# Two graph layers on one core: layer 1 of 20 row blocks moves beside the last product, its late rows listed on the chip

## The chip, the core and the metric

The kernel runs on one core of a Trainium2 chip. A core has five engines that run side by side, each through its own list of instructions in order: TensorE (PE, with its weight loads shown as PEld), VectorE (DVE), ScalarE (ACT), GpSimd (POOL) and SyncE (SP), which here only issues transfers. An engine waits for another through semaphores. 16 DMA engines move data between device memory and the on-chip memory (SBUF); results of TensorE land in PSUM. The metric is the time of one launch on the device, in microseconds (us).

## The reference, cut to what matters

```
x   : 2708 x 512, adj : 2708 x 2708 (about 0.3% of the entries, and the diagonal, are not zero; values 0.05 to 1)

# layer 0
d   = rowsum(adj) ** -0.5
out = relu( (d[:,None] * adj * d[None,:]) @ x @ W + b )
h   = layernorm(x + out)

# layer 1 (4 heads, then their mean)
xn     = h @ W_node + b_node
feats  = einsum('nd,hdf->hnf', xn, K)
logits = s[:, :, None] + (-1e10) * (1 - adj)        # s is one number for each head and row
attn   = softmax(logits, over the columns)
out    = mean over heads of (attn @ feats)
y      = layernorm(h + relu(out))
```

In layer 1 the term with -1e10 decides the softmax: where the largest entry of a row of adj stands clear of the next, the weight of its column is 1 and all others are 0, for every head. Row i of attn @ feats is then feats[j], where j is the column of the largest entry of row i. With M = W_node times the mean of K over the heads, row i of layer 1 is u[j] with u = h @ M + c, so the layer is a gather of rows of u.

## The kernel before, in words

The 2708 rows are split into two halves of 1354, and each half into 10 blocks of 128 rows and one of 74. Block `ib` is part `ib // 2` of half `ib % 2`, so there are 22 blocks; blocks 20 and 21 have 74 rows. "Late" rows below are those of blocks 20 and 21: positions 1280 to 1353 of each half.

**Setup** (up to about 120 us): all of adj and x is loaded, x @ W is formed block by block (`v`), row sums are taken, and M (`m_sb`) and c (`c_bc`) are built from W_node, K and b_node.

**Main loop.** The product adj @ v is made two row blocks at a time. `m` (0 to 10) counts the pairs, `k` (0 to 10) the pairs of column blocks, and one step (m, k) does, in the order in which it is written out by hand (`manual_schedule`; nothing is reordered):
- `ahead(i + 2)`: four transposes of adj blocks for the step after the next (line 289), a copy out of PSUM on ACT (L291), four sums on DVE (L296 to L299). So the sums of a step are needed two steps later.
- `products(i)`: seven products of 128x256 (L318), instead of eight, into four PSUM banks.
- on DVE one piece of `todo`: the layer norm of the pair before (`rows_1`, `rows_2`, `rows_3`), or `scan`, which finds the largest entries of half a row block and their positions (L379, L380).
- at k = 7 and 8 the finished rows h of the pair before are transposed (`turn`), and after the last k `combine` puts the seven products together and `store_u` multiplies h of the pair before by M (L162, 16 matmul records a block pair) and stores u to device memory (`u_d`).

`rows_2` sends the variance to POOL, which adds epsilon and raises to -0.5 (L366, L367), and `rows_3` waits for it.

**After the loop** the last pair (blocks 20 and 21) goes through `rows_1` to `rows_3`, `turn` and `store_u`. A small matmul sums the flags of rows whose maximum does not stand clear (L491); if there were any, a dense version of layer 1 would run at the end. Then layer 1 proper runs for all 22 blocks: POOL issues one indirect transfer for each block, which fetches the rows u[j] (`fetch_row`, L508); DVE applies relu and adds h (L518), takes the statistics (L520, L521); POOL raises four columns at a time to -0.5 (`spread`, L526); ACT normalizes (L536) and SP stores the block to the output. The h of blocks 0 to 9 is read back from device memory (`reload_h`) at the second step of the last pair, that of blocks 10 to 19 after the loop. The column numbers j (`indices`) are computed on DVE at k = 8 of the last pair.

Of the kernel before, what the change touches and what calls it, by code (L numbers as in the profile page):

```python
# [44 lines left out]
GAP = -200.0  # L46


@with_exitstack
def tile_two_graph_layers(  # L50
# [26 lines left out]
    SHORT = rows(NB - 1)  # L77

# [27 lines left out]

    nc.sync.dma_start(out=w_sb, in_=W.rearrange("(c p) o -> p c o", p=P))
# [3 lines left out]
    half_neg = const.tile([P, 4], F32, name="half_neg")  # L111
# [10 lines left out]
    idx = const.tile([P, NB], U32, name="idx")  # L122
    bad_i = const.tile([1, 1], I32, name="bad_i")
    nc.vector.memset(sums, 1.0)
    nc.vector.memset(top, 0.0)
    nc.vector.memset(at, 0)

# [145 lines left out]

    mix = ctx.enter_context(tc.tile_pool(name="mix", bufs=1, side="right"))
# [107 lines left out]
    def store_u(ib):  # L382
        pr = rows(ib)
        po = times(hTs.pop(ib), pr, m_sb)
        ut = mix.tile([P, D], F32, name="ut", bufs=2)
        nc.vector.tensor_add(ut[:pr], po[:pr], c_bc[:pr])  # L386
        store(u_d, ut, ib)

    def indices():


        def col():
            return small.tile([P, NB], F32, name="col", bufs=8)

        v0, v1 = top[:, :, 0, 0], top[:, :, 1, 0]
        best, nxt, tmp = col(), col(), col()
        nc.vector.tensor_tensor(best, v0, v1, op=ALU.max)
        nc.vector.tensor_tensor(nxt, v0, v1, op=ALU.min)
        nc.vector.tensor_tensor(tmp, top[:, :, 0, 1], top[:, :, 1, 1], op=ALU.max)
# [4 lines left out]
        bad = col()  # L404
        nc.vector.memset(bad, 0.0)
        nc.vector.tensor_scalar(bad[:, : NB - 2], nxt[:, : NB - 2], GAP, None, op0=ALU.is_ge)
        nc.vector.tensor_scalar(bad[:SHORT, NB - 2 :], nxt[:SHORT, NB - 2 :], GAP, None, op0=ALU.is_ge)
        bad1 = small.tile([P, 1], F32, name="bad1")
        nc.vector.tensor_reduce(bad1, bad, axis=AX.X, op=ALU.max)
        sel, fa, fb = col(), col(), col()  # L410
        nc.vector.tensor_tensor(sel, v1, v0, op=ALU.is_gt)
        nc.vector.tensor_copy(fa, at[:, :, 0, 0])
        nc.vector.tensor_copy(fb, at[:, :, 1, 0])
        nc.vector.tensor_sub(fb, fb, fa)
        nc.vector.scalar_tensor_tensor(fb, fb, float(HALF), sel, op0=ALU.add, op1=ALU.mult)
        nc.vector.tensor_add(fa, fa, fb)
        nc.vector.tensor_copy(idx, fa)
        return bad1
# [3 lines left out]
    hres = {}  # L422

    def reload_h(lo, hi):
        for ib in range(lo, hi):
            if (ib - lo) % PER == 0:
                hold = apool.tile([P, N], F32, name="a")
            n = (ib - lo) % PER
            hres[ib] = hold[:, n * D : (n + 1) * D]
            load(hres[ib], h_d, ib)  # L430
# [4 lines left out]
    bad1 = None  # L435
    for i, (m, k) in enumerate(steps):
        at_k = i % NM
        if at_k == 0:
            banks = [p_p.tile([P, 2, FH], F32, name=f"bank{n}") for n in range(4)]
            todo = []  # L440
            if done is not None:
                for q in range(2):
                    todo.append([lambda ib=2 * (m - 1) + q, t=done[q]: rows_1(ib, t)])
                    todo.append([lambda ib=2 * (m - 1) + q, t=done[q]: rows_2(ib, t)])
                todo[3].append(lambda ib=2 * (m - 1), t=done[0]: rows_3(ib, t))
                todo.append([lambda ib=2 * (m - 1) + 1, t=done[1]: rows_3(ib, t)])
            look = [(2 * m + 2 + q, hf, 1, q) for q in range(2) for hf in range(2)] if m + 1 < NM else []
# [5 lines left out]
            if m == NM - 1:  # L453
                todo.append([lambda: None])
# [9 lines left out]
        if done is not None and at_k in (7, 8):  # L464
            q = at_k - 7
            hTs[2 * (m - 1) + q] = turn(done[q], rows(2 * m - 2), nc.scalar.copy)
        if m == NM - 1 and at_k == 1:
            reload_h(0, 2 * PER)
        if m == NM - 1 and at_k == 8:
            bad1 = indices()  # L470
# [17 lines left out]
    for q in range(2):  # L488
        store_u(2 * last + q)
# [155 lines left out]
```

## Time and profile before

| | |
|---|---|
| time, median of 3 runs | 696.97 us (695.75 to 698.27) |
| time of the profiled execution | 699.27 us |
| its span, first to last instruction | 697.4 us |
| TensorE busy | 616.2 us, 88% of the span |
| VectorE busy | 462.0 us |
| ScalarE busy | 157.0 us |
| GpSimd busy | 71.6 us |
| last product of the main loop ends | about 613 us |
| first gather is issued | 643.15 us |
| last output store is issued | 692.6 us |

Busy time of an engine is the time in which the profile shows an instruction running on it. An average over the span hides the stages: up to 120 us the transfers are the limit, from there to about 620 us TensorE runs without a gap, and after that it has little to do. The clock that was granted to TensorE is shown as a share of full speed; it is 1 in the main loop and 0.5 in parts of the end.

### The profile page before, as it was taken

How to read it: one execution, taken by the hardware profiler on the slowest of the kernel's cores; microseconds unless marked ns; L12 is line 12 of the kernel's file. 1: busy time of each engine (PE TensorE's matmuls, PEld its weight loads, DVE VectorE, ACT ScalarE, POOL GpSimd, SP SyncE). 2: the span in 40 equal slices, each digit the busy share in tenths (PEclk: the TensorE clock that was granted, in tenths of full speed). 3: DMA queues.
4: the chain of work that ended last, by engine and by line, in shares of the span. 5: the costliest groups of instructions: out<-in, count | busy, mean ns of one | idle time of the engine just before them, and what ended most of it. 6: DMA issues, size and time to landing. Idle time of an engine off the chain costs nothing.

```text
span 697.4 us, 7653 instructions
## 1 busy us (share of the span) xinstructions
PE 616.2 (88%) x2768; PEld 456.6 (65%) x2768; DVE 462.0 (66%) x1116; ACT 157.0 (23%) x221; POOL 71.6 (10%) x102
## 2 busy tenths in 40 slices
PE   5999979999999999999999999999999999965000
PEld 3545434887878878878788788787887876731000
DVE  1356886998776856858659578586595775350693
ACT  2544455211111211211111112111121111100054
POOL 0011321000001001000010000000100001010771
PEclk9999999999999999999999999999999999986555
DMA  8999799013050230400513204014041105013785
GB/s 350 412 391 404 299 360 338 1 63 128 30 205 30 108 128 31 189 32 32 204 46 141 80 31 190 31 68 182 31 101 53 62 15 188 28 39 101 250 285 182
DMA packets 29892, 101.79 MB, mean 146 GB/s; under 512 B 3904, under 2 KB 3904, under 8 KB 24688
## 3 DMA queue, kind: packets, MB, share of 16 engines
q1 hardware_dynamic: 27608, 95.69, 37.2%
q0 software_dynamic: 2240, 5.55, 2.6%
q8 instruction: 23, 0.38, 0.2%
q14 instruction: 21, 0.17, 0.1%
HBM read 84.59 MB, written 16.64 MB: 145 GB/s over the span
## 4 chain that ended last, share of the span: by engine, by line
PE 78%; DVE 12%; DMA 4%; POOL 3%; issue 1%; ACT 1%; SPq 0%
PE bank L318 48%; PE po L162 21%; PE tp L289 6%; PE tp L154 3%; DMA gt<-u_d,idx 2%; DVE at L380 2%; POOL gt L508 2%; DVE top L379 2%; DVE km L241 1%; DMA v<-in_x_dram 1%; PE po L265 1%; DVE v L181 1%; DVE aT L299 1%; ACT gt L536 1%; DVE st L520 1%
## 5 line engine op out<-in xcount | busy, mean ns | idle before, releaser
L318 PE MATMUL bank<-v,aT 128*128 128x256 f32 (+3 forms) x968 | 268.5, 380 | 0.3 <-DVE t L340 0.3
L318 PE MATMUL bank<-t,aT 128*128 128x256 f32 (+3 forms) x726 | 196.5, 379 | 1.2 <-DVE u L345 0.8
L318 PEld LDWEIGHTS bank<-v,aT 128*128 128x128 f32 (+3 forms) x968 | 170.6, 186 | 22.4 <-DVE t L340 0.6
L318 PEld LDWEIGHTS bank<-t,aT 128*128 128x128 f32 (+3 forms) x726 | 134.8, 186 | 23.7 <-DVE u L345 1.2
L291 ACT COPY aT<-tp 128x512 f32<-128x512 f32 (+3 forms) x121 | 68.9, 570 | 347.9 <-PE tp L289 334.4
L296 DVE TENSOR_TENSOR aT<-aT 128x128 f32<-128x128 f32 (+3 forms) x121 | 33.8, 279 | 88.1 <-ACT aT L291 88.1
L162 PE MATMUL po<-w_sb,sT 128*128 128x512 f32 (+1 forms) x176 | 80.9, 604 | 3.3 <-DVE sT L156 3.3
L162 PE MATMUL po<-m_sb,sT 128*128 128x512 f32 (+1 forms) x176 | 80.2, 610 | 0.0
L289 PE MATMUL tp<-ident,a 128*128 128x128 f32 (+3 forms) x484 | 70.5, 269 | 0.3 <-ACT aT L291 0.3
L379 DVE MAX8 top<-a 128x8 f32<-128x1354 f32 (+1 forms) x44 | 68.8, 1563 | 0.0
L380 DVE FIND_INDEX8 at<-top,a 128x8 uint32<-128x1354 f32 (+1 forms) x44 | 68.7, 1562 | 0.0
L289 PEld LDWEIGHTS tp<-ident,a 128*128 128x128 f32 (+3 forms) x484 | 58.6, 139 | 15.2 <-issue 5.3
L235 ACT ACTIVATE junk<-a 128x2708 bf16<-128x2708 f32 (+1 forms) x22 | 54.1, 2461 | 48.5 <-DMA a<-in_adj_dram 48.5
L162 PEld LDWEIGHTS po<-m_sb,sT 128*128 128x128 f32 (+1 forms) x176 | 33.4, 190 | 40.2 <-issue 39.6
L366 POOL TENSOR_SCALAR rs<-mv 128x1 f32<-128x1 f32 (+1 forms) x22 | 7.5, 342 | 481.0 <-DVE mv L364 481.0
L162 PEld LDWEIGHTS po<-w_sb,sT 128*128 128x128 f32 (+1 forms) x176 | 31.7, 190 | 37.5 <-issue 33.5
L386 DVE TENSOR_TENSOR ut<-po,c_bc 128x512 f32<-128x512 f32 (+1 forms) x22 | 15.2, 691 | 50.8 <-PE po L162 50.8
L233 DVE COPY v<-po 128x512 f32<-128x512 f32 (+1 forms) x22 | 15.2, 690 | 35.3 <-PE po L162 35.3
L299 DVE TENSOR_TENSOR aT<-aT 128x128 f32<-128x128 f32 (+3 forms) x121 | 34.6, 286 | 4.2
L297 DVE TENSOR_TENSOR aT<-aT 128x128 f32<-128x128 f32 (+3 forms) x121 | 33.7, 278 | 0.0
L298 DVE TENSOR_TENSOR aT<-aT 128x128 f32<-128x128 f32 (+3 forms) x121 | 33.7, 278 | 0.0
L175 POOL TENSOR_TENSOR dinv<-dinv,half_neg 128x1 f32<-128x1 f32 x22 | 19.0, 863 | 102.7 <-DVE dinv L174 102.7
(90 smaller groups left out, 372.4 us busy)
## 6 DMA issues: line engine op xcount, KB each, us to landing
a<-in_adj_dram SPq DMA_DIRECT2D x38, 1354.0 KB, 6.1
v<-in_x_dram SPq DMA_DIRECT2D x20, 256.0 KB, 10.5
xr<-in_x_dram SPq DMA_DIRECT2D x20, 256.0 KB, 8.9
h_d<-t SPq DMA_DIRECT2D x20, 256.0 KB, 2.1
u_d<-ut SPq DMA_DIRECT2D x20, 256.0 KB
a<-h_d SPq DMA_DIRECT2D x20, 256.0 KB, 4.5
out_dram<-gt SPq DMA_DIRECT2D x20, 256.0 KB, 3.7
kh<-in_L_gnn_K_dram SPq DMA_DIRECT2D x3, 1024.0 KB
```

The costliest lines, as they stand in the source:

```text
L154: nc.tensor.transpose(ps[:, f, :pr], src[:pr, f * P : (f + 1) * P], ident[:pr, :pr])
L162: nc.tensor.matmul(po[:pr], sT[:, f, :pr], wt[:, f, :], start=(f == 0), stop=(f == ND - 1))
L235: nc.scalar.activation(junk[:pr], a[:pr], AF.Copy, accum_out=sums[:pr, ib : ib + 1])
L289: nc.tensor.transpose(ps[:kr, q, :pr], raw[m][q // 2][:pr, lo : lo + kr], ident[:pr, :pr])
L291: nc.scalar.copy(aT[:kr, :4, :pr], ps[:kr, :, :pr])
L296: nc.vector.tensor_add(s(S1), s(L21), s(L22))
L297: nc.vector.tensor_sub(s(S3), s(L11), s(L21))
L298: nc.vector.tensor_sub(s(S2), s(S1), s(L11))
L299: nc.vector.tensor_sub(s(S4), s(L12), s(S2))
L318: nc.tensor.matmul(banks[bank][:pr, side, :], aT[:kr, left, :pr], right, start=first and side == 0, stop=last, skip_group_check=True,)
L379: nc.vector.max(out=top[:pr, ib, hf, :], in_=part)
L380: nc.vector.max_index(out=at[:pr, ib, hf, :], in_max=top[:pr, ib, hf, :], in_values=part)
```

## The change

Layer 1 of blocks 0 to 19 is done while the last pair (m = 10) is still being multiplied, except for the rows that need a row u[j] of blocks 20 or 21.

- `u` is stored with relu applied (one more ACT instruction a block), and the gather adds to h in place: h of a block is loaded into its place (`home`), and the indirect transfer has `compute_op=add`. The DVE pass L518 is gone. The device tensors `u_d` and `out` are each seen as two views, early and late, which are not ordered against each other.
- At m = 9, `marks` (k = 1) computes the column numbers of blocks 0 to 19, sets the number of a row that needs a late row to 0, and flags it. Two small matmuls count the flags; `ranks` (k = 2) turns the counts into a running number for each flagged row; `enlist` (k = 3 to 7, four blocks a step) makes on POOL a 128x256 matrix with a one at the row's number (`hot`, two buffers) and on TensorE two matmuls of it with a table `about` of each row's coordinates, so that up to 256 rows are listed in PSUM; `listed` (k = 9) turns the list into three columns of addresses: which row of h, which row of u, which row of the output.
- At m = 10 the layer norm of blocks 18 and 19 is drawn together into the first two steps, `turn` comes at k = 2 and `store_u` of 18 and 19 at k = 3. POOL then fetches blocks 0 to 4 at k = 4, 5 to 9 at k = 5, 10 to 14 at k = 7 and reads h of the listed rows at k = 8; DVE takes the statistics of blocks 0 to 4 at k = 7 and of 5 to 9 at k = 9; the first five blocks are normalized and stored at k = 8.
- After the loop come the last pair's layer norm and `store_u`, blocks 15 to 19, then the gathers of blocks 20 and 21 and a second gather for the 256 listed places, whose normalized rows are scattered over the rows that were stored before. Places that stand for no row carry an address past the end and are dropped.
- Before the loop, blocks 20 and 21 of `h_d` and `u_d` are filled with `b_bc`, so that every row can be read.

```diff
+    NE = NB - 2
+    LATE = (NM - 1) * P
+    NL = CAP // P                      # CAP = 256
+    u_early, u_late = dram_disjoint_views(u_d[:, :], 2)
+    out_early, out_late = dram_disjoint_views(out, 2)
...
+    for ib in (NE, NE + 1):
+        for t in (h_d, u_d):
+            store(t, b_bc, ib)
...
         nc.vector.tensor_add(ut[:pr], po[:pr], c_bc[:pr])
-        store(u_d, ut, ib)
+        nc.scalar.activation(ut[:pr], ut[:pr], AF.Relu)
+        store(u_late if ib >= NE else u_early, ut, ib)
...
+    def marks():
+        sel, pos_in, full = indices(0, NE, P)          # 15 DVE operations on 20 columns
+        flag = small.tile([P, NE], F32, name="flag", bufs=1)
+        nc.vector.tensor_scalar(flag, pos_in, float(LATE), None, op0=ALU.is_ge)
+        nc.vector.scalar_tensor_tensor(full, pos_in, float(LATE), full, op0=ALU.is_lt, op1=ALU.mult)
+        nc.vector.tensor_copy(idx[:, :NE], full)
+        nc.vector.tensor_scalar(about[:, :, 3], pos_in, float(LATE), None, op0=ALU.subtract)
+        nc.vector.tensor_copy(about[:, :, 4], sel)
+        flag_b = small.tile([P, NE], BF16, name="flag_b", bufs=1)
+        nc.vector.tensor_copy(flag_b, flag)
+        ps = p_o.tile([P, D], F32, name="po")
+        nc.tensor.matmul(ps[:, :NE], before, flag_b, start=True, stop=True)
+        nc.tensor.matmul(ps[:, NB : NB + NE], every, flag_b, start=True, stop=True)
+        return flag, ps
+    def ranks(flag, ps):
...
+        while shift < NE:                              # 5 rounds
+            a, t = runs[n], runs[1 - n]
+            nc.vector.tensor_add(t[:, PAD:], a[:, PAD:], a[:, PAD - shift : PAD - shift + NE])
...
+    def enlist(rank, ls, bl):
+        for ib in bl:
+            hot = mix.tile([P, CAP], BF16, name="hot", bufs=2)
+            nc.gpsimd.tensor_scalar(hot, place, rank[:, ib : ib + 1], None, op0=ALU.is_equal)
+            for n in range(NL):
+                nc.tensor.matmul(ls[:, n * 6 : n * 6 + 6], hot[:, n * P : (n + 1) * P], about[:, ib, :],
+                    start=(ib == 0 and n == 0), stop=(ib == NE - 1), skip_group_check=True)
...
+    def home(c):                                       # h of five blocks into one buffer
+        t = mix.tile([P, N], F32, name="home") if c == 2 else apool.tile([P, N], F32, name="a")
+        for n, ib in enumerate(range(c * PER, (c + 1) * PER)):
+            gt[ib] = t[:, n * D : (n + 1) * D]
+            load(gt[ib], h_d, ib)
+    def fetch_row(ib):
+        pr = rows(ib)
+        fetch(gt[ib], pr, idx[:pr, ib : ib + 1], u_d if ib >= NE else u_early, compute_op=ALU.add)
+    def chunk_stats(c):                                # DVE: statistics of 5 blocks; POOL: power of 5 columns
+        for ib in range(*chunk(c)):
+            stats(ib, P)
+        spread(*chunk(c))
+    def chunk_out(c):                                  # DVE: shift (waits for POOL); ACT: normalize; SP: store
+        shift_of(*chunk(c))
+        for ib in range(*chunk(c)):
+            normalize(ib, P)
+            store(out_early, gt[ib], ib)
...
+        if m == NM - 2:                                # m = 9, after products() and the todo piece
+            if at_k == 1:
+                flag, ps = marks()
+            elif at_k == 2:
+                rank = ranks(flag, ps)
+                ls = p_o.tile([P, D], F32, name="po")
+            elif 3 <= at_k < 8:
+                per = NE // 5
+                enlist(rank, ls, range((at_k - 3) * per, (at_k - 2) * per))
+            elif at_k == 9:
+                to_read, to_get, to_put = listed(ls)
+        if final:                                      # m = 10
+            if at_k == 0:
+                home(0)
+                home(1)
+            elif at_k == 1:
+                home(2)
+            elif at_k == 2:
+                for q in range(2):
+                    hTs[2 * (m - 1) + q] = turn(done[q], P, nc.scalar.copy)
+            elif at_k == 3:
+                store_u(NE - 2)
+                store_u(NE - 1)
+            elif at_k == 4:
+                sel, pos_in, full = indices(NE, NB, SHORT)
...
+                for ib in range(*chunk(0)):
+                    fetch_row(ib)
+            elif at_k == 5:
...
+                for ib in range(*chunk(1)):
+                    fetch_row(ib)
+            elif at_k == 7:
+                chunk_stats(0)
+                for ib in range(*chunk(2)):
+                    fetch_row(ib)
+            elif at_k == 8:
+                chunk_out(0)
+                for n in range(NL):
+                    gt[NB + n] = mix.tile([P, D], F32, name=f"again{n}")
+                    fetch(gt[NB + n], P, to_read[:, n : n + 1], h_d)
+            elif at_k == 9:
+                chunk_stats(1)
+            elif at_k == 10:
+                home(3)
         if at_k == NM - 1:
-            if done is not None:
-                new = combine(m, banks)
+            new = combine(m, banks)
+            if done is not None and not final:
                 store_u(2 * m - 2)
                 store_u(2 * m - 1)
...
+    chunk_out(1)
+    for q in range(2):
+        rows_1(NE + q, done[q])
+        rows_2(NE + q, done[q])
+    for ib in range(*chunk(3)):
+        fetch_row(ib)
+    for q in range(2):
+        rows_3(NE + q, done[q])
+        hTs[NE + q] = turn(done[q], SHORT, nc.scalar.copy)
+    chunk_stats(2)
+    store_u(NE)
+    first, after = chunk(3)
+    for ib in (first, first + 1):
+        stats(ib, P)
+    store_u(NE + 1)
+    for ib in range(first + 2, after):
+        stats(ib, P)
+    spread(first, after)
+    for q in range(2):
+        gt[NE + q] = done[q]
+        fetch_row(NE + q)
+    for n in range(NL):
+        fetch(gt[NB + n], P, to_get[:, n : n + 1], u_late, compute_op=ALU.add)
+    chunk_out(2)
+    chunk_out(3)
+    for ib in (NE, NE + 1):
+        stats(ib, SHORT)
+    spread(NE, NB)
+    for n in range(NL):
+        stats(NB + n, P)
+    spread(NB, NB + NL)
...
+    for n in range(NL):
+        normalize(NB + n, P)
+        nc.gpsimd.indirect_dma_start(out=out_early[:, :],
+            out_offset=bass.IndirectOffsetOnAxis(ap=to_put[:, n : n + 1], axis=0),
+            in_=gt[NB + n], in_offset=None, bounds_check=N - 1, oob_is_err=False)
```

## The prediction

> **What bounds the kernel now.** I read the stages first (busy time by window: PE, PEld, DVE, ACT, POOL, then TensorE clock, DMA share, GB/s).
>
> ```profile
> 500.00:550.00 50.00, 50.00 (x245) 41.17 (x244) 34.17 (x83) 8.49 (x16) 1.78 (x4) 1.00 0.31 78
> 620.00:640.00 20.00, 11.24 (x26) 4.08 (x26) 7.46 (x15) 0.81 (x2) 2.60 (x4) 0.74 0.17 43
> 640.00:660.00 20.00, 0.00 (x0) 0.00 (x0) 9.33 (x20) 0.00 (x0) 13.19 (x13) 0.50 0.80 265
> 660.00:680.00 20.00, 0.00 (x0) 0.00 (x0) 18.79 (x44) 8.78 (x12) 16.03 (x14) 0.50 0.85 269
> 680.00:698.00 18.00, 0.00 (x0) 0.00 (x0) 5.96 (x16) 7.26 (x10) 2.14 (x2) 0.50 0.50 175
> ```
>
> Until 620 us PE never pauses; in the last 77 us it works 11 us. Then the chain that ended last (start, us, what), in that tail:
>
> ```profile
> 613.00 6.88 PE po L162 x16
> 620.51 0.75 DVE t L354
> 627.82 9.68 PE po L162 x16
> 643.15 7.05 DMA gt<-u_d,idx
> 676.25 9.06 DMA gt<-u_d,idx
> 689.39 2.21 ACT gt L536 x3
> ```
>
> The tail is one chain: layer norm of blocks 20 and 21, their product with M, then 22 gathers that POOL issues from 643.15 to 677.7, then what follows the last. The change attacks this stretch and pays inside the main loop, so I looked up the prices on POOL (busy, mean ns) and two landing times:
>
> ```profile
> L508 POOL DMA_INDIRECT gt<-u_d,idx x22 | 24.5, 1115 | 22.9 <-DMA a<-h_d 16.8 <-issue 6.1
> L366 POOL TENSOR_SCALAR rs<-mv 128x1 f32<-128x1 f32 x20 | 6.5, 324 | 447.3 <-DVE mv L364 447.3
> L526 POOL TENSOR_TENSOR rss<-rss,half_neg 128x4 f32<-128x4 f32 x5 | 6.1, 1227 | 4.3 <-DVE nbs L530 3.8 <-DVE rss L525 0.4
> masks.py:199 POOL TENSOR_SCALAR_AFFINE_SELECT ident<-ident 128x128 f32<-128x128 f32 x1 | 0.3, 293 | 0.1
> masks.py:197 POOL MEMSET ident<- 128x128 f32 x1 | 0.2, 205 | 0.3 <-POOLq L632 0.3
> ```
>
> ```profile
> h_d<-t SPq DMA_DIRECT2D x20, 256.0 KB, 2.1
> gt<-u_d,idx POOLq DMA_INDIRECT x22, 5.0
> ```
>
> Last the timeline at m = 9, for how DVE and PE stand to each other, and the one place where PE paused early:
>
> ```profile
> 537.24 0.18 DVE L364 BATCH_NORM_AGGREGATE mv<-st 128x2 f32<-128x6 f32 x1
> 537.74 0.60 PE L289 MATMUL tp<-ident,a 128*128 128x128 f32 x4
> 541.21 0.60 PE L289 MATMUL tp<-ident,a 128*128 128x128 f32 x4
> ```
>
> ```profile
> 102.95 0.66 PE L251 MATMUL po<-ident,bn 128*128 128x128 f32 x4 [2.67 <-DVE wn L257]
> ```
>
> A step at m = 9 takes 3.46 us, and in step k = 1 DVE is done 0.3 us before PE. Whatever is put behind DVE or POOL in PE's list there stalls PE.
>
> **Parts hidden.** The 20 relus on ACT (0.8 each, row L536) delay ACT's copy at k = 0 by 0.8; the sums made from it are needed two steps (6.9 us) later. The eight fill stores stand on SP before the loads of blocks 2 and 3; 8 x 0.45 us delays them from about 121 to 125 us, and they are first read after 137. POOL's nine constants lie before 5 us; POOL is first needed at 38. If any cover failed it would cost its own 1 to 4 us.
>
> **Part 1, stalls added at m = 9 (+17.0).**
> - `marks`, k = 1: DVE has finished `rows_2` at 537.4. L397 to L417, 18 like operations, took 604.90 to 607.60, 0.15 each; 21 here take 3.15, to 540.6. PE's two counting matmuls stand before the next transposes, and PE was ready at 537.7; with 0.3 for handing over: 3.2.
> - k = 2 and 3, all 3.2 later: DVE's `rows_1` ends at 544.65, `ranks` (13 operations, most waiting for the one before, 0.18) 547.05, the four sums 0.95 to 548.0, `rows_2` 0.8 to 548.85. On POOL L366 and L367 of that block stand ahead of the first `hot`: 1.25, to 550.1. Four `hot` at H each and 0.3: PE goes on at 552.8 for H = 0.6, where its products ended at 547.9: 4.9.
> - k = 4 to 7: two `hot` fill the buffers during the products; the third waits for PE to read the first, the fourth follows: 2H and 0.6 for handing over and eight small matmuls (a transpose takes 0.11): 1.8 x 4 = 7.2.
> - H: no row has a 128x256 compare on POOL. Floor: 0.32 (L366) plus twice the 0.10 that 128 columns add to a memset = 0.53. By the affine select 0.32 + 2 x 0.19 = 0.7. High: L175 on POOL took 0.55 alone and 1.46 beside DVE, so up to 1.1. I take 0.6, nearest to the one-input rows. 12H is in the sum, so 16 to 23.
> - Clock: after the 2.67 us pause of the last fence the granted clock was 0.57 over 104 to 108 us, which is 3.4 us at half: 1.7 lost. The pauses at k = 1 and 3 are about 3 us. The first slow stretch falls into waiting that comes anyway; the second counts: 1.7. Bounds 0 and 5.
>
> The Trainium skill (TensorE: Matmul & The Clock Gate, Part 1) says that the clock halves after an idle window of about 3.4 us; by that the 3 us pauses cost nothing and the sum is 1.7 less. The trace halved after 2.67 us, so I follow the trace. It also (GPSIMD Engine Reference, 3.1 and 4.1) puts elementwise work on VectorE, about twice as fast, and gives 1.03 to 2.6 cycles an element at 1.2 GHz; the estimate from it is 0.54 to 0.87 us for `hot`, 3 us more at its upper end. No row here shows the operation.
>
> **Part 2, until the last layer norm (+5.4).** Times are those of before, with the stalls of part 1 still to be added. m = 10 starts at 576.4. Four steps of 3.28, both `turn` (0.9) and some slack for ACT end at 590.7; `store_u` of 18 and 19 moves here from 613, 6.9 to 597.6. DVE's add 0.7, relu 0.8, issue 0.3, landing 2.1 (row of h_d): u is there at 601.6. POOL then issues ten gathers at 0.95 + 0.30: 614.1; the power of five columns 1.4 (its statistics are ready at 612.7: fifth gather issued at 606.6, landing 5.0, DVE 1.1): 615.5; five gathers and two reads of h: 624.3; second power: 625.7. PE's remaining seven steps end at 620.6 (DVE's sums for the last step are done at 613.6, behind the first statistics, 4 us in hand); `combine` ends at 623.9, since ACT first normalizes five blocks. But `chunk_out(1)` stands on DVE before `rows_1`, and its shift waits for POOL's second power. So `rows_1` starts at 625.9 and not 620.5.
>
> **Part 3, the tail (-36.3).** From `rows_1` (T) to the end it was 697.4 - 620.5 = 76.9. After: to the add for block 21 as before 17.7 (same half clock), relu 0.8, issue 0.9, landing 2.1: T + 21.5. Beside it POOL gathers blocks 15 to 19 from T + 5.8 to 12.0, landed 17; DVE takes the last three statistics after the add, T + 20.5; power 1.4: POOL is free at T + 21.9. Four gathers end at 27, the last lands at 30.8; statistics 1.1, power 0.75, shift 0.3, normalize 0.75: first scatter at T + 33.7, second issued by 36.2; from the last issue to the end it took 4.4 before: T + 40.6. The 14 remaining stores on SP lie beside the gathers.
>
> **Part 4, gathers that add (+5.8).** No row shows one. On the path stand 15 before T and 4 behind, each y dearer to issue, and the last landing x later: 19y + x. Low end: a plain gather, 0. High end: issue and landing doubled, y = 1.25, x = 5.0, 28.8, and 6.3 more because blocks 15 to 19 then land too late: 35. Rows and addresses are those of a plain gather, so I stay near that row: y = 0.25, x = 1, inside L508's own spread (0.95 to 1.64 us).
>
> Sum: 697.4 + 17.0 + 5.4 - 36.3 + 5.8 = 689.3, 8.1 below the span. The profiled execution took 699.27, 2.3 above the median 696.97; 697.0 - 8.1 = 689.
>
> **Rivals.**
> - *Slower: the adding gather is dear.* Place: POOL's issue and the landings. It decides from 19y + x = 13.9, for instance y = 0.6 and x = 2.5; with both doubled the span is 683.5 + 35 = 718.5, halfway 705. For it: each row must also be read at its destination, and POOL alone sets T. Against it: DMA is at 0.04 to 0.3 of its share beside the product, so there is room.
> - *The product is stalled more.* H = 1.1 and three slow stretches of 1.7: part 1 becomes 26.4, the time 699. For it: POOL's 1.46 beside DVE. Against it: PE's wait in each step stays below the 1.66 us that did not slow it at 84 us.
> - *It does not hide the gathers.* In the old tail the first gather waited 3.9 us after the last u store, not 2.1, until a read of h had landed. If POOL starts 8 us later than I say, T moves by as much: 697.
> - *Cheaper than I think.* y = x = 0 and part 1 at 14: 680.5.
>
> **Chances.** My forecast (682 to 695) 0.38; cheaper 0.08; stalls or a late start (695 to 702) 0.26, of it 0.08 faster, 0.09 within, 0.09 slower; dear gathers 0.28. A measurement tells about 0.3%, 2.1 us, from no change. Faster 0.54, same 0.09, slower 0.37. The range leaves out the upper half of the dear gathers and the low end of the cheap case: 679 to 710; the forecast's own is 682 to 695.
>
> **What would show it.** PE pauses of about 3 us behind `marks`, 5 behind the first `enlist`, and 1.8 in each of four steps; 17 us more up to m = 10. The issue interval of `fetch_row` against 1.25. DVE's shift before `rows_1` waiting for POOL. No gathers of blocks 0 to 14 after the loop. I am wrong if `hot` takes over 1.1, if an adding gather takes over 1.9 to issue, or if DVE's statistics hold up the sums of the last step.

## The result

The changed kernel takes 714.7 us (median of 4 runs, 714.5 to 715.5); the kernel before, run beside it, takes 697.6 us (4 runs, 695.8 to 699.2). The ratio is 1.0248, with a 95% interval from 1.0219 to 1.0276. The change makes the kernel 17 us slower; the prediction said 8 us faster. The profiled execution has a span of 713.0 us, against 697.4 us before; the sum of the prediction, 689.3 us, was a sum of the span, so there are 23.7 us to be found.

Three marks split the span. Product m = 9 begins at 529.9 us (530.8 before) and takes 69.0 us instead of 45.6. The last layer norm (T in the prediction) begins at 657.6 us; with the 22.5 us by which m = 10 is late taken off this is 635.1 us, where the prediction had 625.9 and, with its share of part 4 (15 x 0.25), 629.7. From T to the end it takes 55.4 us, where the prediction had 40.6 and, with its share of part 4, 42.6. Against the prediction that is +6.4 at m = 9, -0.9 because m = 9 begins sooner, +5.4 until T and +12.8 behind T: 23.7.

The stages of the changed kernel, by window (stretch, its length, PE, PEld, DVE, ACT and POOL busy, granted TensorE clock, DMA share, GB/s):

```profile
500.00:550.00 50.00, 45.81 (x215) 36.81 (x214) 35.85 (x106) 8.34 (x15) 2.87 (x6) 0.97 0.26 65
640.00:660.00 20.00, 3.08 (x15) 1.78 (x13) 9.17 (x26) 6.21 (x10) 15.12 (x11) 0.63 1.02 226
660.00:680.00 20.00, 10.48 (x24) 3.87 (x24) 13.21 (x32) 4.71 (x8) 12.89 (x11) 0.67 0.86 221
680.00:700.00 20.00, 0.00 (x0) 0.00 (x0) 2.40 (x7) 5.83 (x9) 8.53 (x5) 0.50 0.68 173
```

PE was busy for all 50 us of the first window before; now it pauses. The gathers did move out of the tail, but the last 70 us still hold little TensorE work (10.6 us; before, 11 us in the last 77), and between 680 and 700 us TensorE does nothing and DVE works 2.4 us: it waits for gathers to land.

The timeline of PE at m = 9 in the changed kernel (start, us, what; in brackets the idle time before it and what ended that):

```profile
539.48 0.18 PE L471 MATMUL po<-flag_b,before 128*128 128x20 bf16 x1 [2.50 <-DVE flag_b L469]
539.53 1.10 PE L332 MATMUL tp<-ident,a 128*128 128x128 f32 x4
544.65 0.60 PE L332 MATMUL tp<-ident,a 128*128 128x128 f32 x4
549.97 0.20 PE L504 MATMUL po<-about,hot 128*128 128x6 bf16 x2 [1.69 <-POOL hot L502]
552.74 0.78 PE L332 MATMUL tp<-ident,a 128*128 128x128 f32 x4
559.26 0.20 PE L504 MATMUL po<-about,hot 128*128 128x6 bf16 x2 [1.10 <-POOL hot L502]
560.15 0.20 PE L504 MATMUL po<-about,hot 128*128 128x6 bf16 x2 [0.69 <-POOL hot L502]
560.22 0.64 PE L332 MATMUL tp<-ident,a 128*128 128x128 f32 x4
566.02 0.64 PE L332 MATMUL tp<-ident,a 128*128 128x128 f32 x4
573.50 1.05 PE L332 MATMUL tp<-ident,a 128*128 128x128 f32 x4
581.43 0.61 PE L332 MATMUL tp<-ident,a 128*74 128x128 f32 x4
```

The L332 lines are the first transposes of the steps, so their distances are the lengths of the steps: k = 2 takes 5.12 us, k = 3 8.09, k = 4 7.48, k = 5 5.80, k = 6 7.48, k = 7 7.93 (with one `turn`), where a step took 3.46 before. The waits stand where the prediction put them: 2.5 us behind `marks`, then the four `hot` of k = 3 (1.69 and three times 0.7), and two waits in each later step, some 13.5 us in all. With the small matmuls and the handing over between them they make the steps 16.7 us longer. Four steps ran at half the clock (k = 2, 4, 6 and 7; four transposes at the start of a step then take up to 1.1 us instead of 0.6), which adds 1.66 us each, 6.65 in all.

The price list of POOL (line, operation, count | busy, mean ns of one | idle before):

```profile
L546 POOL DMA_INDIRECT a<-u_d,idx x15 | 23.6, 1573 | 21.4 <-PE tp L332 17.6 <-issue 3.3 <-DMA a<-h_d 0.3
L502 POOL TENSOR_SCALAR hot<-place,rank 128x256 bf16<-128x256 f32 x20 | 18.1, 927 | 14.2 <-PE po L504 14.2
L546 POOL DMA_INDIRECT t<-u_d,idx x2 | 4.7, 2338 | 0.5 <-issue 0.5
L546 POOL DMA_INDIRECT again<-h_d,to_read x2 | 2.0, 984 | 0.6 <-issue 0.6
```

An adding gather of 128 rows takes POOL 1.57 us, a plain one (the last line, same kernel) 0.98; with 74 rows the adding one takes 2.34. One `hot` takes 0.93 us.

The timeline from T to the end, thinned:

```profile
657.48 0.17 DVE L566 SCALAR_TENSOR_TENSOR nbs<-mvs,rss 128x5 f32<-128x5 f32 x1 [5.93 <-POOL rss L562]
657.56 0.74 DVE L397 SCALAR_TENSOR_TENSOR t<-t,dinv,b_bc 74x512 f32<-74x512 f32 x1
680.02 2.38 POOL L546 DMA_INDIRECT t<-u_d,idx  x1 [0.20 <-issue]
693.38 0.69 DVE L556 BATCH_NORM_STATS2 st<-t 74x6 f32<-74x512 f32 x1 [13.36 <-DMA t<-u_d,idx]
698.01 0.69 DVE L556 BATCH_NORM_STATS2 st<-t 74x6 f32<-74x512 f32 x1 [3.73 <-DMA t<-u_d,idx]
704.54 1.08 POOL L720 DMA_INDIRECT out_dram<-again,to_put  x1 [1.84 <-ACT again L570]
708.27 1.00 POOL L720 DMA_INDIRECT out_dram<-again,to_put  x1 [2.65 <-issue]
```

T waits for DVE's shift, and that for POOL's second power, as foretold. The late gathers start at T + 22.5 us, also as foretold (21.9). But the gather of block 20, issued at 680.0, is read only 13.4 us later, and the second scatter stands 2.65 us behind the first.

### The profile page after: what moved, and what is told of

Its sections match the earlier page's. It is cut to its first block, busy times and chain, and to the rows that moved or that the text cites. A ratio compares the mean times of both kernels' runs of the same rounds, so it can differ in the third digit from the quotient of the medians.

```text
span 713.0 us, 7893 instructions
## 1 busy us (share of the span) xinstructions
PE 625.0 (88%) x2810; PEld 462.8 (65%) x2810; DVE 455.4 (64%) x1142; ACT 170.9 (24%) x245; POOL 110.2 (15%) x135
## 5 line engine op out<-in xcount | busy, mean ns | idle before, releaser
L361 PE MATMUL bank<-v,aT 128*128 128x256 f32 (+3 forms) x968 | 271.9, 384 | 0.4 <-DVE t L383 0.4
L361 PE MATMUL bank<-t,aT 128*128 128x256 f32 (+3 forms) x726 | 199.0, 383 | 1.2 <-DVE u L388 0.8
L361 PEld LDWEIGHTS bank<-v,aT 128*128 128x128 f32 (+3 forms) x968 | 172.9, 189 | 23.3 <-DVE t L383 0.6
L361 PEld LDWEIGHTS bank<-t,aT 128*128 128x128 f32 (+3 forms) x726 | 136.9, 189 | 24.7 <-DVE u L388 1.2
L339 DVE TENSOR_TENSOR aT<-aT 128x128 f32<-128x128 f32 (+3 forms) x121 | 33.7, 279 | 96.4 <-ACT aT L334 96.3
L332 PE MATMUL tp<-ident,a 128*128 128x128 f32 (+3 forms) x484 | 71.9, 272 | 0.5 <-ACT aT L334 0.3
L332 PEld LDWEIGHTS tp<-ident,a 128*128 128x128 f32 (+3 forms) x484 | 58.5, 140 | 15.4 <-issue 5.8
L342 DVE TENSOR_TENSOR aT<-aT 128x128 f32<-128x128 f32 (+3 forms) x121 | 34.7, 287 | 4.2
L430 ACT ACTIVATE ut<-ut 128x512 f32<-128x512 f32 (+1 forms) x22 | 13.8, 629 | 97.1 <-DVE ut L429 97.1
L340 DVE TENSOR_TENSOR aT<-aT 128x128 f32<-128x128 f32 (+3 forms) x121 | 33.7, 279 | 0.0
```

Of the source, the lines that this page charges most:

```text
L332: nc.tensor.transpose(ps[:kr, q, :pr], raw[m][q // 2][:pr, lo : lo + kr], ident[:pr, :pr])
L339: nc.vector.tensor_add(s(S1), s(L21), s(L22))
L340: nc.vector.tensor_sub(s(S3), s(L11), s(L21))
L342: nc.vector.tensor_sub(s(S4), s(L12), s(S2))
L361: nc.tensor.matmul(banks[bank][:pr, side, :], aT[:kr, left, :pr], right, start=first and side == 0, stop=last, skip_group_check=True,)
```

## The experiments

The theory after the result: the listing stalls PE through `hot` and the halved clock; an adding gather is dear on POOL; and gathers of 74 rows land very late. The rivals: at m = 9 the small matmuls themselves cost the time; in the tail the output stores that go out beside the late gathers hold them up. Each set of runs has the kernel before beside it, and that took 696.8 to 698.3 us from set to set; a difference between runs of different sets is therefore good to about 1 us, and the ratio to the kernel before is the safer figure.

**Four buffers for `hot`.**

```
-            hot = mix.tile([P, CAP], BF16, name="hot", bufs=2)
+            hot = mix.tile([P, CAP], BF16, name="hot", bufs=4)
```

> Changed kernel with four buffers for `hot` in place of two. Theory: the waits at m = 9 come from the two buffers. With four, POOL makes the four tiles of a step (0.90 us each) during the 3.46 us of products, so the steps k = 4 to 7, which took 5.8 to 7.5 us, should take about 4.1 (products and eight small matmuls); k = 3, where POOL only starts after the power of rows_2, stays near 8.1. These four steps were 14.4 us above normal and keep about 2.8: 11.6 us faster than the changed kernel, about 703. Rival: the small matmuls among the products, not the waits, bring the half clock and most of the loss; then only the waits of 1.8 a step go, 7 us at most, about 708, and the granted clock at m = 9 stays at 0.83 to 0.89.

Measured: 703.5 us, ratio to the kernel before 1.0093 (1.0069 to 1.0118), 11.2 us faster than the changed kernel. PE at m = 9, the step k = 2 and then k = 4 to 6:

```profile
539.22 0.17 PE L471 MATMUL po<-flag_b,before 128*128 128x20 bf16 x1 [2.49 <-DVE flag_b L469]
539.27 0.63 PE L332 MATMUL tp<-ident,a 128*128 128x128 f32 x4
542.76 0.60 PE L332 MATMUL tp<-ident,a 128*128 128x128 f32 x4
551.83 1.09 PE L332 MATMUL tp<-ident,a 128*128 128x128 f32 x4
557.41 0.64 PE L332 MATMUL tp<-ident,a 128*128 128x128 f32 x4
561.32 0.64 PE L332 MATMUL tp<-ident,a 128*128 128x128 f32 x4
```

The steps fall to 5.6 us (k = 4, still at half the clock) and 3.9 (k = 5), with the same matmuls in them. So the rival falls: the waits cost, the eight small matmuls about 0.4 us a step. Steps k = 2 and 3 together take 12.6 us here and 13.2 in the changed kernel, though k = 2 ran at half the clock in the changed kernel alone.

The clock gives a surprise. Nearly the same pause behind `marks`, 2.49 us here and 2.50 in the changed kernel, is followed by a step of 3.49 us at full speed here and by one of 5.12 us there.

**Listing matmuls two steps later.** `hot` keeps its place on POOL and has eight buffers, the counting matmuls move from k = 1 to 2 and the address list from k = 9 to 10.

```
-            elif 3 <= at_k < 8:
-                enlist(rank, ls, range((at_k - 3) * per, (at_k - 2) * per))
+            if 3 <= at_k < 8:
+                mark_hot(rank, range((at_k - 3) * per, (at_k - 2) * per))
+            if 5 <= at_k < 10:
+                enlist(ls, range((at_k - 5) * per, (at_k - 4) * per))
```

> Changed kernel with the counting matmuls one step later (k = 2), eight buffers for `hot`, and the listing matmuls two steps behind the POOL comparisons they read (k = 5 to 9). Theory: nobody on TensorE waits any more; m = 9 falls from 69.0 us to about 47.5 (45.6 before the change and 42 small matmuls), the granted clock stays at about 1, the rest of the kernel is moved as a whole: 21 us faster than the changed kernel, about 693.5, some 4 below the kernel before. Rival: the work on POOL and DVE beside each other slows the sums that TensorE needs, and m = 9 stays above 52 us; then about 699.

Measured: 695.5 us, ratio 0.9967 (0.9953 to 0.9982). m = 9 takes 48.4 us (530.95 to 579.36), and the clock is 1.00 in every 20 us window from 500 to 600 us; one of them, in the order of the windows above:

```profile
540.00:560.00 20.00, 19.44 (x116) 16.95 (x116) 18.31 (x55) 2.93 (x5) 13.19 (x14) 1.00 0.15 53
```

In the changed kernel itself the clock of this stretch is 0.84, and 0.83 in the next 20 us:

```profile
540.00:560.00 20.00, 14.58 (x67) 11.78 (x66) 7.78 (x31) 1.76 (x3) 8.16 (x10) 0.84 0.17 53
```

19.2 us come back from an edit that removes no work. With it the change would just have paid for itself.

**No list at all.** The two counting matmuls and the branches for k = 2 to 7 are left out, and `to_read`, `to_get`, `to_put` are filled with constants, so that the rows that need a late row keep a wrong value and the scatters drop all they carry.

> Changed kernel that lists nothing: no counting, ranking or listing at m = 9 (the rows that need a late row keep a wrong value), constant addresses in the four gathers and two scatters of listed rows. It prices the whole of the listing. Theory: m = 9 is again 45.6 us and the program 23.4 us shorter: about 691.3. Rival: part of the 23.4 us comes from what else the change puts beside m = 9; then it stays above 693.

Measured: 692.6 us, ratio 0.9944 (0.9927 to 0.9960). m = 9 takes 45.5 us (531.27 to 576.81), as before the change. The listing costs 22.1 us in the changed kernel (21 by the ratios); with its matmuls two steps later 2.9 us of that are left, with two waits of 0.6 us among them, so some 19 us come from where it was put.

**80 rows in the late gathers.** Rows 74 to 79 are cleared and get a row nobody uses.

```
-        pr = rows(ib)
+        pr = 80 if ib >= NE else P
         fetch(gt[ib], pr, idx[:pr, ib : ib + 1], ...)
```

> Changed kernel with the adding gathers of blocks 20 and 21 made of 80 rows in place of 74 (six rows of no use, cleared beforehand). Theory: the two gathers land late (13.4 and 15.3 us after their issue, and the two listed gathers behind them 14.2 and 13.6) because 74 rows are cut into many small packets; with 80 they land like the others, in 6 to 7 us, the last statistics come some 7 us sooner, about 707.5. Rival: the ten output stores of 256 KB that are issued beside them fill the DMA engines; then the landings stay at 12 us and more and the time within 1.5 us of the changed kernel's 714.7.

Measured: 708.0 us, ratio 1.0153 (1.0133 to 1.0173), 6.7 us faster than the changed kernel. The same two gathers and their readers:

```profile
679.65 1.50 POOL L549 DMA_INDIRECT t<-u_d,idx  x1 [0.17 <-issue]
681.46 1.45 POOL L549 DMA_INDIRECT t<-u_d,idx  x1 [0.30 <-issue]
684.72 0.69 DVE L559 BATCH_NORM_STATS2 st<-t 74x6 f32<-74x512 f32 x1 [5.03 <-DMA t<-u_d,idx]
687.61 0.69 DVE L559 BATCH_NORM_STATS2 st<-t 74x6 f32<-74x512 f32 x1 [1.99 <-DMA t<-u_d,idx]
```

The first is read after 5.1 us (13.4 with 74 rows) and the second after 6.2 (15.3), although the ten output stores still go out beside them: contention with the stores alone falls as the cause. What differs shows in the DMA view of the changed kernel over the late gathers (680 to 702 us) and then in that of the kernel with 80 rows (679 to 695 us). In the first line of each, every digit is the busy share of the 16 DMA engines in tenths, for one fortieth of the stretch:

```profile
DMA  3999995989675989999999965333232111110000
DMA packets 2944, 3.46 MB, mean 157 GB/s; under 512 B 1260, under 2 KB 1260, under 8 KB 2944
```

```profile
DMA  0039999988999999799999899999999995100000
DMA packets 1920, 3.47 MB, mean 217 GB/s; under 512 B 224, under 2 KB 224, under 8 KB 1920
```

The bytes are the same; with 74 rows there are some 1,040 more packets under 512 B, and most of them come first: from 682 to 688 us the gathers of the changed kernel send 993 packets that hold 0.08 MB (with 80 rows 219 packets and 0.38 MB from 681 to 688). The data follows, and it comes slowly: the share is 0.22 from 696 to 698 us and 0.14 from 698 to 700, which is at most 3.5 and 2.2 of 16 engines, while with 80 rows it stays near full until almost all has landed. So the run shows that the number of rows makes the late landing; whether the small packets or the few engines cost the time it does not show.

The Trainium skill (DMA: Bandwidth & Descriptors, "Why a DMA increments its semaphore by 16 and not by 1") says that a transfer is spread over the largest number of engines, up to 16, that divides its outermost dimension, here the rows. By that rule it would be 2 engines for 74 rows and 16 for 80, an estimate that fits the falling share; no run here shows the engines one by one.

**Plain gathers, with 74 and with 80 rows.** The keyword `compute_op=ALU.add` is taken out of both `fetch` calls, so that h is missing from the output.

> Changed kernel with plain gathers everywhere, which leave out the addition of h (the residual of layer 1 is missing from the output). It prices the addition by itself. Theory: a gather is issued in 0.95 + 0.30 us in place of 1.54 + 0.30; POOL then no longer sets the start of the last layer norm, which falls by 6 us to the end of `combine`; the four late gathers save 2 us of issue and the 74-row ones land about 4.5 us sooner, with half the packets: 12.5 us faster than the changed kernel, about 702. Rival: the late landings are contention with the output stores and stay; then about 706.5.

> Late gathers of 80 rows, and plain gathers everywhere (the addition of h is left out), to be held against the run with 80 rows alone (708.0). The run with plain gathers and 74 rows (700.9) mixed the price of the addition with that of the small packets. Theory: the addition by itself costs 4 us at the start of the last layer norm and 0.6 us in each of four late gathers with a little of their landing, 8 us in all: about 700, hardly less than with 74 rows, since plain 74-row gathers land in 8.8 us and only some 1 to 2 us of it are on the path. Rival: most of what the plain gathers saved was the packets of the 74 rows; then the addition costs 3 to 4 us and this run shows about 704.5.

Measured: 700.9 us with 74 rows (ratio 1.0052, 1.0036 to 1.0067) and 699.1 with 80 (1.0033, 1.0021 to 1.0046). Adding therefore costs 13.8 us with 74 rows and 8.9 with 80 (708.0 - 699.1); 74 rows in place of 80 cost 1.8 us with plain gathers (1.3 by the ratios) and 6.7 with adding ones. POOL's price list with plain gathers of 74 rows, to be held against the one above:

```profile
L546 POOL DMA_INDIRECT a<-u_d,idx x15 | 14.7, 980 | 21.4 <-PE tp L332 17.3 <-issue 3.7 <-DMA h_d<-t 0.3
L546 POOL DMA_INDIRECT t<-u_d,idx x2 | 2.8, 1392 | 0.6 <-issue 0.6
```

The rival expectation of the second run (3 to 4 us for the addition) falls. T came 4.0 us sooner with plain gathers (653.6), not 6: the matmuls of the last step paused several times for 0.4 to 1.1 us with no recorded cause, and `combine` ended 2 us later (653.6 against 651.6). Why they paused is open. POOL's second power itself ended at 649.3 us, 626.0 with the delay of m = 10 in that run (23.3 us) taken off.

**The order around the last layer norm.** First `chunk_out(1)` was put behind it, and the two reads of h for listed rows behind its powers:

```
-    chunk_out(1)
     for q in range(2):
         rows_1(NE + q, done[q])
         rows_2(NE + q, done[q])
+    for n in range(NL):
+        fetch(gt[NB + n], P, to_read[:, n : n + 1], h_d)
     ...
+    chunk_out(1)
     chunk_stats(2)
```

> Changed kernel with `chunk_out(1)` put behind the last layer norm (DVE and ACT) and the two plain gathers of listed rows of h put on POOL behind that layer norm's two powers. Theory: the last layer norm starts late only because DVE's shift in front of it waits for POOL; it starts at the end of `combine`, 6 us sooner (relative to the loop), its scaling 5.7 us sooner, and the gathers of blocks 15 to 19 3 us sooner, as two gathers of 1.25 now stand before them. The late gathers stand on POOL behind the power of blocks 15 to 19 and so gain only these 3 us: about 711.7. Rival: the late gathers wait for the stores of u for blocks 20 and 21, not for POOL; then all of 5.7 us is gained, about 709. Second rival: POOL is the only limit all through, and nothing is gained: 714.7.

Measured: 718.6 us, ratio 1.0315 (1.0273 to 1.0357): 3.9 us slower, which neither side had expected. The timeline shows what it could come from:

```profile
651.48 0.75 DVE L397 SCALAR_TENSOR_TENSOR t<-t,dinv,b_bc 74x512 f32<-74x512 f32 x1
657.39 0.69 DVE L400 SCALAR_TENSOR_TENSOR t<-t,xr 74x512 f32<-74x512 f32 x1 [5.16 <-DMA xr<-in_x_dram]
669.70 2.19 SPq L101 DMA_DIRECT2D h_d<-t  x4
678.12 2.75 SPq L101 DMA_DIRECT2D u_d<-ut  x4
```

The layer norm did start 6 us sooner, but its second operation needs x, and that load stands on SP behind the output stores of blocks 0 to 4, which wait for ACT. It lands at 657.4, the very time at which POOL let T go. And the stores of h for blocks 20 and 21 (669.7, 664.1 in the changed kernel) now come after the gathers that read h; the stores of u stand behind them and behind five output stores. Moreover these two gathers of h now stand on POOL before the gathers of blocks 15 to 19, which start at 665.3 us instead of 663.6. Two more runs take part of this away: the loads of x issued at k = 4 of m = 10 instead of k = 9, alone, and with `chunk_out(1)` moved but the reads of h left where they were.

> Changed kernel in which the two loads of x for the last pair are issued four steps earlier in m = 10, ahead of the output stores of blocks 0 to 4 on SP. Theory: the start of the last layer norm has two causes that end together, POOL's second power (657.5) and this load of x (657.4 in the run with the changed order); taking away the load alone leaves POOL's: within 1.5 us of 714.7. Rival: the load was the limit and the shift that waits for POOL only stood beside it; then up to 4 us faster.

> Changed kernel with both: the loads of x four steps earlier, and `chunk_out(1)` behind the last layer norm; the gathers of listed rows of h stay where the change has them. Theory: only together do they let the last layer norm start at the end of `combine`, about 651.5 in place of 657.5; its two powers then stand behind POOL's second power and end 3 us sooner than before; the gathers of blocks 15 to 19 and the late ones move by the same 3 us: about 711.7. Rival: the stores of blocks 5 to 9, now behind that layer norm, come between the stores of h and of u on SP and give the 3 us back: about 714.7.

Measured: 715.8 us (ratio 1.0248, 1.0231 to 1.0265) and 714.9 us (1.0240, 1.0223 to 1.0258). The load alone gains nothing, as expected. With both, the last layer norm starts at 650.9, but the time does not move, as the rival had it:

```profile
650.94 0.75 DVE L397 SCALAR_TENSOR_TENSOR t<-t,dinv,b_bc 74x512 f32<-74x512 f32 x1
659.46 1.68 POOL L546 DMA_INDIRECT a<-u_d,idx  x1 [0.17 <-issue]
666.89 5.52 SPq L101 DMA_DIRECT2D out_dram<-a  x5
672.51 2.54 SPq L101 DMA_DIRECT2D u_d<-ut  x4
678.87 2.38 POOL L546 DMA_INDIRECT t<-u_d,idx  x1 [0.65 <-issue]
```

The gathers of blocks 15 to 19 start 4.1 us sooner than in the changed kernel (663.6), the late ones 1.2 us sooner (680.0): two things give the rest back. The gathers land later, beside the five output stores: the last one is read 8.9 us after its issue, 6.3 in the changed kernel, so that POOL's power of blocks 15 to 19 ends only 1.6 us sooner. And the five output stores stand before the stores of u on SP, and the first late gather waits 0.65 us behind that power, 0.20 in the changed kernel.

**A free second scatter.** It writes through a view of its own, so that it does not wait for the first.

```
-    out_early, out_late = dram_disjoint_views(out, 2)
+    out_early, out_late, out_again = dram_disjoint_views(out, 3)
```

> Changed kernel in which the second scatter of listed rows writes through a view of its own, so that it needs not wait for the first to land (their rows are disjoint). Theory: the 2.65 us that POOL waits between the two scatters go and the program ends 2.4 us sooner, about 712.3. Rival: what ends the program is the landing of the other output stores, and nothing changes.

> Late gathers of 80 rows, and the second scatter through a view of its own. With 74 rows the free second scatter showed only 0.8 us, though POOL's wait of 2.65 us was gone, while the late gathers happened to land 2.4 us later in that profile. Theory: without the scattered landings of the 74-row gathers the 2.4 us show: 705.6. Rival: the second scatter then lands later, beside the first, and less than 1 us is gained: 707.3.

Measured: 713.9 us with 74 rows (ratio 1.0234, 1.0194 to 1.0274), 0.8 us less than the changed kernel, which is not told from nothing; 706.6 us with 80 rows (1.0146, 1.0130 to 1.0163), 1.4 us less than without the view, but only 0.5 by the ratios, whose intervals overlap. POOL's wait falls from 2.63 us to 0.30 in the second pair of runs:

```profile
699.60 1.00 POOL L723 DMA_INDIRECT out_dram<-again,to_put  x1 [0.30 <-issue]
```

From the end of that issue to the end of the span it then takes 4.2 us (704.8 - 700.6), against 3.7 with the wait, so part is given back. The wait, then, was for the first scatter, and without it 0.5 to 1.4 us are gained, nearer to the rival (under 1) than to the theory (2.4).

**A kernel that beats both.** Four edits were put together: listing later and 80 rows, which had helped, and `chunk_out(1)` with the reads of h later and the free scatter, which by themselves gave no clear gain; then step by step the late gathers before POOL's power of blocks 15 to 19; the loads of x early and h in two views; and `combine` with the last layer norm ahead of the normalizing of blocks 0 to 4.

> Four edits at once: the listing as in the run with the matmuls two steps later (measured 19.2 us), 80 rows in the late gathers (6.7 us), the order of the run beside this one (3 us) and the free second scatter (2.4 us). Theory: they touch different stretches and add: 714.7 - 31.3 = 683.4, some 14 below the kernel before. Rival: the gains in the tail overlap, since POOL, the landings and the output stores are each near the limit there; then half of the 12 us in the tail, about 689.5.

> As the run with four edits, and POOL issues the late gathers before the power of blocks 15 to 19, whose normalizing and storing so begin later. Theory: the late gathers start when the u of block 21 has landed, 3 to 4 us sooner, and the output stores of blocks 15 to 19 still land before the scatters: about 680. Rival: these five stores, 7 us later now, hold up the scatter, which must come after them: no gain on the run with four edits.

> The combined kernel with late gathers first (686.7), with the loads of x four steps earlier and with h in two views, so that the stores of h for blocks 20 and 21 need not wait for the gathers of listed rows of h. Theory: in that kernel the first late gather waited 8.1 us for the store of u, which stood on SP behind the store of h (held up by the gathers of h until 649.2) and five output stores; now u is there some 9 us sooner: about 677.7. Rival: POOL's chain of 20 gathers of 1.85 us and three powers is the limit right behind, and only 3 us are gained: 683.5.

> As the run beside it, and `combine` of the last pair stands ahead of the normalizing of blocks 0 to 4 and the statistics of blocks 5 to 9, so that it starts when TensorE ends (about 624) and not 5 us later; two gathers of blocks 10 to 14 go behind the last layer norm's powers. Theory: the last layer norm and all behind it come 4 us sooner, about 674. Rival: POOL, which has the same gathers to issue, is the limit by now, and the time is that of the run beside it.

Measured, in this order: 688.2 us (ratio 0.9874, 0.9835 to 0.9912), 686.7 (0.9845, 0.9808 to 0.9883), 682.9 (0.9779, 0.9763 to 0.9796) and 678.1 (0.9714, 0.9698 to 0.9730). The first is near its rival: 26.5 us below the changed kernel, where listing later and 80 rows alone had given 25.9, so the new order and the free scatter added next to nothing. The second and third gained less than hoped, 1.5 and 3.7 us, near what their rivals had; in the third the first late gather still waited 5.7 us for the store of u. The last came 4.9 us below the third, near what its theory had (4). It is 20.2 us (2.9%) below the kernel before, measured beside it (698.3), and has T at 625.7 and the first late gather at 651.5:

```profile
625.67 0.75 DVE L401 SCALAR_TENSOR_TENSOR t<-t,dinv,b_bc 74x512 f32<-74x512 f32 x1
670.29 1.07 POOL L740 DMA_INDIRECT out_dram<-again,to_put  x1 [5.85 <-DMA out_dram<-t]
```

What ends it now is the scatter, which waits 5.9 us for output stores, as the rival of the run with the late gathers first had it. Plain gathers with the addition on DVE, as the kernel before has them, were not tried.

## Why the prediction was wrong

The forecast had the sign wrong. What happened is its first rival, the dear adding gather, together with a good part of the second, the stalls. (The 705 that the prediction gives for "halfway" does not come out of its figures: the middle between 683.5 and 718.5 is 701.) The term that failed most is the price of the adding gather, but no single term turns the sign: with part 4 as foretold the time would be 706.7, with part 1 as foretold too 700.3. In the run with plain gathers, held against the prediction's own sum without part 4 (683.5), 15.3 us are still missing: 6.3 until m = 10, 4.4 until T and 4.6 behind T.

- **Part 4, the adding gather (5.8 foretold).** This step failed. The prediction had no row for it and took y = 0.25 us, "so I stay near that row"; the trace has 1.57 against 0.98, y = 0.6. With y = 0.6 the prediction's own sum for T gives 629.7 + 15 x 0.35 = 634.9; measured, 635.1. With plain gathers POOL's second power ended at 626.0, where the prediction had 625.7. So the chain on POOL was right and its price was not. The term x was meant for one late landing and set to 1. The whole cost 13.8 us by the run with plain gathers, 8.0 more than foretold; the rival's own threshold, 13.9 for 19y + x, was near.
- **Part 3, the late gathers (landing about 6 us).** The 74-row gather was mis-sized although its row was on the page: the prediction showed the last 74-row gather landing after 9.1 us and then counted it like one of 128 rows, 5.0 and x. The 1.64 us at the upper end of L508's spread, to which it pointed for y, is also a 74-row gather; those of 128 rows take 0.95 to 1.31. Adding made the landings 13.4 and 15.3. The run with 80 rows puts 6.7 us on the 74 rows; 4.9 of it (6.7 - 1.8) are inside the 13.8 above. The second scatter was counted with its issue alone; its wait of 2.65 us is worth 0.5 to 1.4.
- **Part 1, the stalls at m = 9 (17.0 foretold; 16 to 23 by H, and the clock 0 to 5 in place of 1.7).** Their places and kinds were right; m = 9 became 23.4 us longer. H was 0.93 us, not 0.6: just above the upper end of the estimate that the prediction worked out from the Trainium skill (GPSIMD Engine Reference, 3.1 and 4.1), 0.54 to 0.87. A step of k = 4 to 7 lost 2.3 us besides the clock, where the sum had 1.8; with H = 0.93 the prediction's own 2H + 0.6 gives 2.5. The clock was the larger miss: four slow steps, 6.65 us, where 1.7 was taken and 5 was the bound. That the first slow stretch falls into waiting that comes anyway was largely right: its 1.66 us cost only about 0.65, by the kernel with four buffers.
- **Part 2 (T at 625.9).** The limit named, the shift that waits for POOL, is the limit. Not seen was a second one at the same place: the load of x on SP, behind output stores that the change had put before it. It cost nothing here, but it hid what removing the first would give. `combine` too ended 5 us later than the 623.9 foretold (651.6 - 22.5), as ACT first normalizes five blocks, which wait for POOL's first power; in the run with plain gathers that power was early, but the pauses of TensorE held `combine` and so T, 4.4 us later than foretold.
- **Parts hidden.** m = 9 begins 0.9 us sooner than before, so the relus until then, the fill stores and the constants cost nothing that shows.
- **The gathers hide.** They do: ten of them are issued between 624.7 and 643.2 us beside the product. The first starts at 602.2 us with the 22.5 taken off, where the prediction had 601.6, and without the list the change is 0.6% faster than the kernel before. The rival of a late start is out.

## What to carry to other kernels

A new operation that stands many times on the path should not be given the price of the row it looks most like: the adding gather took 1.57 us to issue where the plain one took 0.98, and it stood there 19 times. A shape that has a row of its own, like the 74-row gather, should be priced by that row. Small helpers in a stream that never paused belong behind the work they wait for by a step or two; the same list cost 22 us in place and 3 us two steps later. Before an order is changed, each queue has to be read for what stands behind the moved piece, SP's stores above all.

## What the runs showed that was not expected

- Two pauses of 1.1 and 0.7 us at the end of a step, with tiny matmuls between them, came four times (k = 4 to 7). Half the clock followed twice (steps k = 6 and 7) and full speed twice (k = 5 and 8). One pause of 2.5 us was followed by half the clock in one kernel and not in another. The Trainium skill (TensorE: Matmul & The Clock Gate, Part 1) says that activity is watched in a free-running window of about 3.4 us, so that the effect changes from run to run. Its idle window of that length does not show in these pauses, which are all shorter; that equal pauses have unequal effects does.
- A gather of 74 rows cost POOL 2.34 us to issue with addition and 1.39 without, one of 80 rows 1.48 and 0.94, and one of 128 rows 1.57 and 0.98. Six rows more were cheaper.
- A store to one part of a DRAM tensor waited for a gather that reads another part while both went through one view: the stores of h of blocks 20 and 21 came 5.6 us later when the gathers of h were moved in front of them. With h in two views they were issued at 639.8 us, during those gathers, instead of 649.2 in the kernel before that edit (the loads of x came earlier there too).
